# Attention in sets of four row groups, layer norm's deviations in two parts, and a load with a buffer for every piece

## The chip, the cores and the metric

The kernel runs on one core of one Trainium2 chip. The metric is the device time of one execution in microseconds. All arithmetic on the path here is in 32-bit floats, and a matmul of such operands appears in the profile as two records, one for each pass.

## The reference

The input x has 256 rows, 256 columns and 32 channels. Four layers follow each other, each preceded by a group norm over 16 groups of channels, and each adds its result to x.

```python
# layer 0: attention whose softmax weights sum to 1 over an axis that v lacks,
# so that what is left of it is the gated v
mn = (m - mu) * rsqrt(var + LN_EPS) * ln_gamma + ln_beta     # over the 32 channels
v = mn @ Wv                      # 32 -> 256
g = sigmoid(mn @ Wg)             # 32 -> 256
x = x + (g * v) @ Wo + bo
# layers 1 and 2: 3x3 mean, then the size of the Sobel gradient
x = x + sqrt(gx * gx + gy * gy + 1e-6)
# layer 3: two stacked LSTM-like cells with a group norm of their gates,
# along 256 time steps (the second axis) for 256 sequences (the first)
zz = group_norm(concat(z, h) @ W_cell + b_cell); i, f, o, g = split(zz)
c = sigmoid(f) * c + sigmoid(i) * tanh(g); h = sigmoid(o) * tanh(c)
x = x + (gn_x + z @ W_out + b_out)    # gn_x: x after its group norm, fed to the cells
```

## The kernel before

The image lies in SBUF as `xa`: 128 partitions are 4 columns of the image times 32 channels (the four "row groups" j of 32 partitions), and along the free axis there are 64 blocks of 256 rows of the image. Two blocks make a pair of 512 elements, `pair(t, k)`; there are 32 pairs k.

**Load** (L208 to L256). The image comes in eight pieces of 32 columns, each two DMAs of 512 KB on SP's queue into one of three `nat` buffers. PE transposes each into four PSUM tiles (L240), ACT copies them to `xa` (L247) and DVE takes the statistics (L248). Before the last piece's transposes PE computes the biases and the centred weights of `wv4` and `wg4` (L221, L233); these need the weights times gamma, which POOL computes (L230). POOL also fills `avg` (L193). In this part the order on each engine is the scheduler's: DMAs and small operations of later code (the recurrence's weights `wc`, a reduction L755) are moved forward into it. Group norm then aggregates the statistics (L159), averages them over channels with small matmuls, among junk matmuls (`busy`), and yields `less` (minus the mean) and the scale.

**Layer norm** (L281 to L337). Each pair is shifted by `less` into `xb`, half of them on DVE and half on POOL (L288). Eight groups g of four pairs follow: PE centres them with sixteen 32x32 matmuls (L306), ACT squares them (L316), and PE sums the squares of the group before into one bank `pvar` (L292). After the last group ACT takes the root (L322) and DVE its reciprocal, `rstd` (L324). Row k of it must be spread over 32 partitions for pair k. For pairs 0 to 2 a matmul does that (L334); for the others `rows_of` (L267) issues four DMAs on SP's queue, from one partition to 32 each, into one of four `rows` buffers, and POOL multiplies (`scaled`, L279).

**Attention** (L344 to L467). One step per pair k, 32 in all, written out by hand: `plan` gives each operation a time, the operations of all pairs are sorted by k times `step` plus that time, and each engine issues its own in that order. For every row group j and half u of the 256 outputs there are a `g` and a `v` matmul (L393, 32 rows by 128 columns of the array, so that four row groups can run side by side), a sigmoid `sg` on ACT (L402) and a product `mu` on DVE (L406) into a buffer `o`. Then `pr`, eight matmuls of 128 rows by 32 columns (L419), projects back; `r` adds the bias on ACT (L434), POOL adds to `xa` (L435), and `bn` takes statistics on DVE (L438). All PSUM tiles come from one list of eight free banks, taken in the order in which they were released; `sg` has 7 buffers and `o` 14. The centring of the recurrence's weights (L755 to L762) and `spread_out`, which calls `rows_of`, are strewn into the same order.

```python
todo = [
    (k * step + when, one_of, (o, u, j, k)) for k in range(NST) for when, o, u, j in plan
]
```

**The rest.** Two Sobel layers (L479) and the recurrence (L926) follow. The Sobel layers begin with a group norm that takes in junk matmuls too (L516). `RecurrentWeights.rest` (L716) loads the last small weights and computes a few selector columns on DVE (L734 to L743). Ahead of the recurrence there is a group norm with three junk matmuls before, two between and three after its two small matmuls, and then six more at `px` (L1107); after that come its first `zz` matmuls (L992, L995).

Of the kernel before, what the change touches and what calls it, by code (L numbers as in the profile page):

```python
# [33 lines left out]
K_GN, K_CEN = 0, 1  # L34
K_AVG, K_SOBEL = 0, 1
# [26 lines left out]
def net_kernel(  # L62
# [32 lines left out]
    xb = big2.tile([P, NB, S], F32, name="xb")  # L95

# [4 lines left out]
    kt = big2.tile([P, NK - 2, P], F32, name="kt")  # L101
    nc.scalar.dma_start(out=kt, in_=consts[:, 2:NK, :])
# [17 lines left out]
    gamma4 = per_channel(ln_gamma, "gamma4")  # L120
    beta4 = per_channel(ln_beta, "beta4")
# [3 lines left out]
    def four_times(w, n, name):  # L125
        t = big2.tile([P, n], F32, name=name)
        for j in range(J):
            nc.gpsimd.dma_start(out=t[j * C : (j + 1) * C, :], in_=w)
        return t

    wv4 = four_times(w_v, D, "wv4")
    wg4 = four_times(w_g, D, "wg4")
# [23 lines left out]
    def group_norm(stats, psum, before, after, rhs=None):  # L156
# [6 lines left out]
        busy(psum, 2, rhs)  # L163
# [27 lines left out]
    nc.gpsimd.memset(avg, 0.0)  # L191
    for g in range(GROUPS):
        nc.gpsimd.tensor_copy(avg[:, g, g, :], kt[:, K_AVG, 0:P:C])  # L193
    FIRST = 3
    spread = mp.tile([P, FIRST, P], F32, name="spread")
    nc.gpsimd.memset(spread, 0.0)
    for j in range(J):
        rows = slice(j * C, (j + 1) * C)
        nc.gpsimd.tensor_copy(
            spread[rows, :, rows],  # L200
            ident[rows, j * C : j * C + FIRST].unsqueeze(2).to_broadcast([C, FIRST, C]),
        )

    flag = cp.tile([1, 1], mybir.dt.int32, name="flag")
    stats = new_stats()
    WL = 32  # L208
    with tc.tile_pool(name="nat", bufs=3) as natp, tc.tile_pool(
        name="ps_in", bufs=4, space=PSUM  # L210
    ) as ps_in:
        norm_test(tc, natp, flag, gn_gamma, gn_beta)
        for w0 in range(0, T, WL):
            nat = natp.tile([P, 2, WL, C], F32, name="nat")
            for h in range(2):
                nc.sync.dma_start(out=nat[:, h], in_=x_nat[:, h, w0 : w0 + WL, :])
            if w0 == T - WL:
                pbias = ps_in.tile([P, 2, 2, P], F32, name="pt")
                for i, w in enumerate((wv4, wg4)):
                    for half in range(2):  # L220
                        nc.tensor.matmul(  # L221
                            pbias[:, i, half, 0:1],
                            lhsT=w[0:C, half * P : (half + 1) * P],
                            rhs=beta4[0:C, :],
                            start=True,
                            stop=True,
                        )
                nc.scalar.copy(wbias, pbias[:, :, :, 0:1].rearrange("p i h o -> p i (h o)"))
                for w in (wv4, wg4):
                    nc.gpsimd.tensor_scalar(w, w, gamma4, None, ALU.mult)  # L230
                    pw = ps_in.tile([P, 2, 2, P], F32, name="pt")
                    pw = pw[:, 0].rearrange("p h s -> p (h s)")
                    nc.tensor.matmul(pw, lhsT=kg[:, K_CEN, :], rhs=w, start=True, stop=True)  # L233
                    nc.scalar.copy(w, pw)
            for b2 in range(WL // (2 * J)):
# [12 lines left out]
                nc.vector.bn_stats(stats[:, blk // 2, :], dst)  # L248
# [5 lines left out]
        nc.vector.tensor_scalar(cen, kg[:, K_CEN, :], gn[0], None, ALU.mult)  # L254
        for w in (wv4, wg4):
            nc.scalar.activation(w, w, AF.Copy, scale=gn[0])  # L256

# [20 lines left out]
    with tc.tile_pool(name="lnq", bufs=12) as lnq:  # L281
# [47 lines left out]
        with tc.tile_pool(name="ps_sp", bufs=FIRST, space=PSUM) as ps_sp:  # L329
# [6 lines left out]
            for k in range(FIRST, FIRST + 3):  # L336
                scaled(k)  # L337
# [871 lines left out]
```

## Time and profile before

| | us |
|---|---|
| median of 3 runs | 2568.68 |
| lowest, highest | 2567.36, 2572.03 |
| profiled execution, its own time | 2571.38 |
| profiled execution, span | 2569.3 |

| stretch of the span | from, to |
|---|---|
| load | 0 to 38.9 |
| group norm | 38.9 to 45.4 |
| layer norm up to its last variance matmul | 45.4 to 67.1 |
| deviation, its reciprocal, first rows | 67.1 to 75.3 |
| attention | 75.3 to 348 |
| two Sobel layers | 348 to 602 |
| last group norm, start of the recurrence | 602 to 615 |
| recurrence | 615 to 2569 |

PE is busy 98% of the span, DVE 89%, ACT 88%, POOL 53%. A line of the profile gives the engine (PEld loads weights for PE; SPq, POOLq are queues), the line of the kernel, the tile written and the tiles read, shapes and durations. In brackets stands how long the engine sat idle before, and what it waited for.

### The profile page before, as it was taken

The page shows a single profiled execution, that of the slowest core. Times are in us where ns is not written, and L with a number is a line of the kernel's source. Part 1 is how long each engine was busy: PE and PEld are TensorE (multiplying, and loading weights), DVE is VectorE, ACT ScalarE, POOL GpSimd, SP SyncE. Part 2 cuts the span into 40 slices and gives each one's busy share as a digit, 9 for nine tenths or more (in the row PEclk, how much of TensorE's full clock was granted, in tenths as well). Part 3 has the DMA queues.
Part 4 walks back from the last instruction along what each step waited for, and adds up shares of the span by engine and source line. Part 5 has one row for each costly group of instructions (what it writes and reads, how often), then busy time and mean ns, then how long its engine had stood idle before and what let it go on. Part 6 is the DMA issues. An engine that isn't in the chain of part 4 may idle for free.

```text
span 2569.3 us, 41531 instructions
## 1 busy us (share of the span) xinstructions
PE 2510.2 (98%) x11605; PEld 1094.3 (43%) x11605; DVE 2274.3 (89%) x6623; ACT 2254.0 (88%) x6876; POOL 1350.1 (53%) x1387
## 2 busy tenths in 40 slices
PE   7899999998999999999999999999999999999997
PEld 4444445564444444444444444444444444444442
DVE  6577779796999999999999999999999999999996
ACT  5577757675999999999999999999999999999996
POOL 5233358683555555555555555555555555555553
PEclk9999999998999999999999999999999999999998
DMA  4776000002000101010101010100101010100000
GB/s 166 42 42 33 5 1 1 1 1 50 5 15 11 22 5 21 5 21 5 21 5 22 5 21 9 22 14 12 21 5 22 5 22 5 22 5 5 5 5 11
DMA packets 116441, 46.20 MB, mean 18 GB/s; under 512 B 76724, under 2 KB 109653, under 8 KB 116200
## 3 DMA queue, kind: packets, MB, share of 16 engines
q1 hardware_dynamic: 114020, 42.15, 11.7%
q8 instruction: 95, 1.56, 0.2%
q14 instruction: 146, 1.20, 0.2%
q10 hardware_dynamic: 1380, 0.99, 0.1%
q0 software_dynamic: 800, 0.30, 0.0%
HBM read 10.63 MB, written 8.39 MB: 7 GB/s over the span
## 4 chain that ended last, share of the span: by engine, by line
PE 96%; DMA 1%; DVE 1%; issue 1%; ACT 1%; POOL 0%; SPq 0%; DVEq 0%; POOLq 0%; ACTq 0%
PE zz L1027 36%; PE zz L1022 17%; PE zz L995 9%; PE pg L603 8%; PE pa L393 8%; PE pt L1079 5%; PE zz L992 3%; PE pa L419 2%; PE pt L1075 2%; PE px L1124 1%; PE px L1114 1%; PE pg L516 1%; DMA nat<-in_x_dram 1%; PE pc L306 0%; PE pvar L292 0%
## 5 line engine op out<-in xcount | busy, mean ns | idle before, releaser
L1043 POOL TENSOR_TENSOR rs<-ve,mhalf 128x4 f32<-128x4 f32 x1024 | 1031.0, 1007 | 922.7 <-DVE ve L1040 922.7
L1027 PE MATMUL zz<-wc,hT 128*128 128x512 f32 x2040 | 1059.4, 607 | 1.0 <-DVE hT L1085 1.0
L1016 ACT ACTIVATE ga<-zz,rs 128x128 f32<-128x128 f32 x3072 | 972.7, 377 | 39.3 <-POOL rs L1043 10.2
L1040 DVE TENSOR_REDUCE ve<-sq 128x4 f32<-128x516 f32 x1024 | 704.4, 688 | 29.2 <-ACT sq L1035 8.5
L1035 ACT ACTIVATE sq<-zz 128x512 f32<-128x512 f32 x1024 | 629.2, 614 | 38.5 <-PE zz L1027 16.3
L1022 PE MATMUL zz<-wc,hT 128*128 128x512 f32 x1024 | 525.0, 594 | 0.0
L1027 PEld LDWEIGHTS zz<-wc,hT 128*128 128x128 f32 x2040 | 328.6, 190 | 398.9 <-DVE c L1071 167.6
L1016 ACT ACTIVATE go<-zz,rs 128x128 f32<-128x128 f32 x1024 | 393.9, 385 | 0.0
L1063 DVE TENSOR_TENSOR c<-ga 128x128 f32<-128x128 f32 x1024 | 300.1, 293 | 61.8 <-ACT ga L1016 35.2
L1071 DVE TENSOR_TENSOR c<-c,fc 128x128 f32<-128x128 f32 x1020 | 288.9, 283 | 9.0
L1067 DVE TENSOR_TENSOR fc<-ga,c 128x128 f32<-128x128 f32 x1020 | 292.9, 287 | 2.7 <-ACT ga L1016 2.7
L995 PE MATMUL zz<-fx,xt 32*128 32x512 f32 x2048 | 265.6, 588 | 0.0
L402 ACT ACTIVATE sg<-pa,wbias 128x512 f32<-128x512 f32 x256 | 168.9, 687 | 89.5 <-PE pa L393 47.7
L406 DVE SCALAR_TENSOR_TENSOR o<-pa,wbias,sg 128x512 f32<-128x512 f32 x256 | 177.5, 746 | 60.5 <-PE pa L419 46.2
L1079 PEld LDWEIGHTS pt<-ident,c 128*128 128x128 f32 x512 | 71.0, 139 | 284.9 <-DVE c L1071 275.9
L393 PE MATMUL pa<-xb,wv 32*128 32x512 f32 x512 | 181.3, 615 | 8.7 <-DVE o L406 8.1
L393 PE MATMUL pa<-xb,wg 32*128 32x512 f32 x512 | 171.3, 638 | 0.8 <-DVE xb L335 0.8
L1082 ACT ACTIVATE th<-c 128x128 f32<-128x128 f32 x512 | 166.2, 325 | 0.4 <-DVE c L1071 0.4
L1082 ACT ACTIVATE th<-pt 128x128 f32<-128x128 f32 x512 | 145.9, 285 | 18.9 <-PE pt L1079 18.9
L1022 PEld LDWEIGHTS zz<-wc,hT 128*128 128x128 f32 x1024 | 161.2, 197 | 2.8 <-issue 0.5
L1085 DVE TENSOR_TENSOR hT<-pt,th 128x128 f32<-128x128 f32 x512 | 146.3, 286 | 15.8 <-ACT th L1082 15.7
L1075 PEld LDWEIGHTS pt<-ident,go 128*128 128x128 f32 x512 | 71.5, 140 | 202.5 <-ACT go L1016 202.0
(186 smaller groups left out, 2962.8 us busy)
## 6 DMA issues: line engine op xcount, KB each, us to landing
xt<-xa SPq DMA_DIRECT2D x256, 64.0 KB, 2.0
nat<-in_x_dram SPq DMA_DIRECT2D x16, 512.0 KB, 7.9
out_dram<-st SPq DMA_DIRECT2D x252, 32.0 KB, 1.7
rows<-rstd SPq DMA_DIRECT2D x116, 64.0 KB, 6.4
wc<-in_L_conv_W_cell_dram SPq DMA_DIRECT2D x2, 512.0 KB, 8.1
kt<-in_consts_dram ACTq DMA_DIRECT2D x1, 704.0 KB, 7.8
kg<-in_consts_dram ACTq DMA_DIRECT2D x1, 128.0 KB, 4.7
wv<-in_L_conv_Wv_dram POOLq DMA_DIRECT2D x4, 32.0 KB, 5.6
```

The lines of the kernel that those rows point to most:

```text
L393: nc.tensor.matmul(take((o, u, j, k)), lhsT=w[rows, u * P : (u + 1) * P], rhs=pair(xb, k)[rows], start=True, stop=True,)
L995: nc.tensor.matmul(v["zz", l, h, t], lhsT=inputs.of(t, r), rhs=fx[r, :], start=False, stop=l == 0 and t == 0,)
L1016: nc.scalar.activation(dst, gates(x, g), func, scale=scale)
L1022: nc.tensor.matmul(get("zz"), lhsT=v["hT", 0, t][:, seqs], rhs=wc[:, l, 0, :], start=False, stop=t == 0)
L1027: nc.tensor.matmul(get("zz"), lhsT=v["hT", l, t - 1][:, seqs], rhs=wc[:, l, 1, :], start=False, stop=True,)
L1035: nc.scalar.activation(sqs[l, h, t % 2][:, :, 0:H], four(get("zz")), AF.Square, scale=float(H**-0.5))
L1040: nc.vector.tensor_reduce(ve, sqs[l, h, t % 2], AX.X, ALU.add)
L1043: nc.gpsimd.tensor_tensor(rs, get("ve"), inputs.mhalf, ALU.pow)
L1063: nc.vector.tensor_mul(c, gates(get("ga"), 0), gates(get("ga"), 2))
L1067: nc.vector.tensor_mul(fc, gates(get("ga"), 1), get("c"))
L1071: nc.vector.tensor_add(c, c, get("fc"))
L1082: nc.scalar.activation(th, get("pt")[:, 1, 0:P] if turned else get("c"), AF.Tanh)
```

## The change

- **Load.** The image comes in two pieces of 16 and seven of 32 columns, each with a buffer of its own, all issued at once; `xb` is given the memory afterwards. Gamma, beta, `wv4` and `wg4` are loaded by SP after the fourth piece, `kt` and a separate `mean_of` after the last. POOL clears `avg`, fills it from `mean_of`, and then multiplies the weights by gamma. The weights' products (`weights`) come before the last two pieces. From here to the end of attention every engine issues in the order of the program text.
- **Group norm.** The chain is written out with fewer small operations; the pair 2 is shifted by ACT.
- **Layer norm.** DVE shifts all other pairs. The variance has two parts: groups 0 and 1, and groups 2 to 7. The deviation of the first is taken amid the squares of group 3, its reciprocal `rstds[0]` serves pairs 0 to 7, and rows 0 to 2 are sent at once, by DMA as all others; pair 0 is scaled by DVE. `spread` and its matmuls go. The test of gamma and beta (`norm_test`) moves here.
- **Attention.** A new plan with a step of 5.9 has `g` and `v` in sets of four row groups, the projection in two halves `pr` and `pb`, 8 buffers `sg`, 11 `o` and 3 `rows`; `spread_out` and `scaled` have other times. The weights of the recurrence are loaded after layer norm.
- **Seams.** The selector columns move into the first Sobel layer, the centring of the weights adds a negative mean in place of subtracting, and there are fewer junk matmuls ahead of the recurrence.

```diff
-    WL = 32
-    with tc.tile_pool(name="nat", bufs=3) as natp, tc.tile_pool(
-        name="ps_in", bufs=4, space=PSUM
+    front = ExitStack()
+    front.enter_context(tc.manual_schedule())
+    WIDTHS = [16, 16] + 7 * [32]
...
+        for i, wl in enumerate(WIDTHS):
+            name, bufs = ("nat", 7) if wl == 32 else ("half", 2)
+            nat = natp.tile([P, 2, wl, C], F32, name=name, bufs=bufs)
+            nats.append((nat, w0, wl))
             for h in range(2):
-                nc.sync.dma_start(out=nat[:, h], in_=x_nat[:, h, w0 : w0 + WL, :])
...
+                nc.sync.dma_start(out=nat[:, h], in_=x_nat[:, h, w0 : w0 + wl, :])
+            w0 += wl
+            if i == 3:
+                for t, v in ((gamma4, ln_gamma), (beta4, ln_beta)):
...
+                for t, w in ((wv4, w_v), (wg4, w_g)):
+                    for j in range(J):
+                        nc.sync.dma_start(out=t[j * C : (j + 1) * C, :], in_=w)
+        nc.sync.dma_start(out=kt, in_=consts[:, 3:NK, :])
+        mean_of = mp.tile([P, P], F32, name="mean_of")
+        nc.sync.dma_start(out=mean_of, in_=consts[:, K_AVG, :])
+        gb = norm_weights(tc, mp, gn_gamma, gn_beta)
+        nc.gpsimd.memset(avg, 0.0)
+        for g in range(GROUPS):
+            nc.gpsimd.tensor_copy(avg[:, g, g, :], mean_of[:, 0:P:C])
+        scaled_w = []
+        for w in (wv4, wg4):
+            scaled_w.append(mp.tile([P, D], F32, name="wgam", bufs=2))
+            nc.gpsimd.tensor_scalar(scaled_w[-1], w, gamma4, None, ALU.mult)
...
+            if i == len(nats) - 3:
+                weights()
...
+        less = small.tile([P, 1], F32, name="less")
+        nc.vector.tensor_scalar_mul(less, pm, -1.0)
...
+        busy(ps_gn, 3)
+        nc.scalar.activation(pair(xb, 2), pair(xa, 2), AF.Identity, bias=less)
+        gstd = small.tile([P, 1], F32, name="gstd")
+        nc.scalar.activation(gstd, pv, AF.Sqrt, bias=gn_eps)
+
+        def shifted(k):
+            nc.vector.tensor_scalar(pair(xb, k), pair(xa, k), one, less, ALU.mult, ALU.add)
+
+        shifted(0)
+        shifted(1)
...
+        nc.vector.tensor_scalar(cen, kg[:, K_CEN, :], scale, None, ALU.mult)
+        shifted(3)
...
+    EARLY = 2
+    rstds = [lnp.tile([P, 2 * S], F32, name=f"rstd{i}") for i in range(2)]
...
-            for k in range(NST):
-                e = nc.gpsimd if k % 2 else nc.vector
-                e.tensor_scalar(pair(xb, k), pair(xa, k), one, less, ALU.mult, ALU.add)
...
+                if g == 0:
+                    for k in range(J, NST - J):
+                        shifted(k)
                 sqs = []
-                for pc in pcs:
+                for j, pc in enumerate(pcs):
+                    if g == EARLY + 1 and j == 2:
+                        std = deviations()
+                        nc.vector.reciprocal(rstds[0], std)
+                        for k in range(3):
+                            rowsets[k] = rows_of(k)
+                        for k in range(NST - J, NST):
+                            shifted(k)
+                        norm_test(tc, mp, flag, gb)
+                        for k in range(3):
+                            scaled(k)
                     sqs.append(lnq.tile([P, 2 * S], F32, name="sq"))
                     nc.scalar.activation(sqs[-1], pc, AF.Square)
...
-    rw = RecurrentWeights(tc, cells, w_cell, b_cell)
+    rw = RecurrentWeights(tc, cells, one, w_cell, b_cell)
     stats = new_stats()
-    step = 6.6
+    step = 5.9000
     plan = [
...
+        (0.0000, "g", 1, 1),
+        (0.8334, "sg", 1, 1),
+        (2.9800, "g", 0, 1),
+        (3.7879, "sg", 0, 1),
+        (5.9100, "g", 1, 0),
+        (7.0264, "sg", 1, 0),
+        (7.4050, "g", 0, 0),
+        (8.3528, "sg", 0, 0),
+        (8.8600, "v", 0, 0),
+        (8.8700, "g", 0, 2),
+        (9.7954, "sg", 0, 2),
+        (10.3250, "v", 1, 2),
+        (10.3350, "v", 1, 1),
+        (10.3450, "v", 1, 0),
+        (10.3550, "g", 1, 3),
+        (10.5787, "mu", 0, 0),
+        (11.5740, "sg", 1, 3),
+        (11.5795, "mu", 1, 0),
+        (11.8200, "v", 0, 3),
+        (11.8300, "g", 1, 2),
+        (12.9473, "mu", 1, 1),
+        (13.2750, "v", 0, 1),
+        (13.2850, "g", 0, 3),
+        (13.2950, "v", 0, 2),
+        (13.9836, "sg", 1, 2),
+        (13.9933, "mu", 1, 2),
+        (14.0771, "mu", 0, 2),
+        (14.3106, "sg", 0, 3),
+        (14.4469, "mu", 0, 1),
+        (14.7500, "v", 1, 3),
+        (15.3906, "mu", 0, 3),
+        (16.2340, "mu", 1, 3),
+        (17.9944, "pr", 0, 0),
+        (19.6839, "pb", 0, 0),
+        (20.2213, "r", 0, 0),
+        (22.5883, "bn", 0, 0),
...
+            elif o in ("pr", "pb"):
+                half = o == "pb"
+                po = held["po", k][1] if half else take(("po", k))
+                for i in range(J):
+                    nc.tensor.matmul(
+                        po[i * C : (i + 1) * C, :],
+                        lhsT=wo[:, half, :],
+                        rhs=sbuf.pop(("o", half, i, k)),
+                        start=not half,
+                        stop=half,
+                    )
...
+        for k in range(3, NST):
+            todo.append(((k - 2) * step + 4.0, scaled, (k,)))
+            todo.append(((k - 5) * step + 4.5, spread_out, (k,)))
...
-    stats = sobel_layer(xa, xb, stats, 7, 16, [])
+    stats = sobel_layer(xa, xb, stats, 7, 16, [rw.selectors])
...
-        gn = group_norm(stats, ps_n, 3, 3)
+        gn = group_norm(stats, ps_n, 1, 0, 3)
...
-    at(-1e5, busy, 6)
+    at(-1e5, busy, 2)
```

`RecurrentWeights.__init__` stands unchanged in what it issues: two DMAs of 512 KB for `wc` on SP's queue, then POOL clears `bc`, then a DMA on SP's queue writes one row of it.

## The prediction

> **What bounds the kernel now.** I read the busy shares by stretch first: where does an engine run full, and where does none? Columns: stretch, length, then busy us of PE, PEld, DVE, ACT and POOL, the granted PE clock, DMA share, GB/s.
>
> ```profile
> 0.00:38.90 38.90, 25.72 (x141) 21.23 (x141) 22.82 (x36) 19.57 (x37) 19.05 (x52) 0.96 0.74 273
> 38.90:45.40 6.50, 3.94 (x18) 3.12 (x19) 5.74 (x14) 2.66 (x5) 3.05 (x4) 0.95 0.01 3
> 45.40:67.10 21.70, 21.65 (x320) 5.07 (x320) 11.12 (x13) 16.41 (x32) 11.76 (x13) 0.86 0.01 3
> 75.30:111.00 35.70, 27.47 (x148) 13.15 (x148) 16.77 (x27) 19.17 (x30) 8.83 (x7) 0.93 0.83 49
> 111.00:344.00 233.00, 232.49 (x1372) 108.68 (x1373) 180.55 (x267) 165.35 (x257) 79.08 (x76) 0.99 0.47 26
> 615.00:2560.00 1945.00, 1930.98 (x8242) 786.02 (x8242) 1806.25 (x5912) 1847.64 (x6175) 1031.00 (x1024) 1.00 0.07 13
> ```
>
> The recurrence (last row) is three quarters of the span and keeps its code; only its start is touched. So the change lives in the first 348 us. In attention PE looks full, but DVE and ACT are at 77% and 71%. Next, the waits there, and one step in order of time:
>
> ```profile
> DVE o L406 <- PE pa L419: 44.0, 28, 1.6
> ACT sg L402 <- DVE o L406: 40.2, 29, 10.3
> ...
> 201.87 4.89 DVE L406 SCALAR_TENSOR_TENSOR o<-pa,wbias,sg 128x512 f32<-128x512 f32 x7 [1.59 <-PE pa L419]
> 202.65 1.34 ACT L402 ACTIVATE sg<-pa,wbias 128x512 f32<-128x512 f32 x2 [1.08 <-DVE o L406]
> 207.10 0.74 DVE L406 SCALAR_TENSOR_TENSOR o<-pa,wbias,sg 128x512 f32<-128x512 f32 x1
> 207.76 0.68 DVE L438 BATCH_NORM_STATS2 stats<-xa 128x6 f32<-128x512 f32 x1
> 208.95 1.92 PE L419 MATMUL pa<-o,wo 128*32 128x512 f32 x16
> 210.03 4.89 DVE L406 SCALAR_TENSOR_TENSOR o<-pa,wbias,sg 128x512 f32<-128x512 f32 x7 [1.59 <-PE pa L419]
> ```
>
> Once a step DVE stops 1.59 us for the projection (L419). I counted the "o" buffers in program order: all 14 are held when "pr" comes, so the next "mu" needs the buffer that its first matmul frees, 1.08 us after it starts (208.95 to 210.03). Likewise "sg" waits 1.08 us for the first "mu" (201.87 to 202.65), as a count of 7 buffers taken in the order in which they are freed gives. That order of reuse is what I walk below. Last, the load's end and the deviations:
>
> ```profile
> 32.17 0.93 POOL L230 TENSOR_SCALAR wv<-wv,gamma 128x256 f32<-128x256 f32 x1 [8.35 <-issue]
> 34.65 3.52 PE L240 MATMUL pt<-ident,nat 128*128 128x128 f32 x16
> 36.80 2.73 DVE L248 BATCH_NORM_STATS2 stats<-xa 128x6 f32<-128x512 f32 x4 [3.20 <-ACT xa L247]
> ...
> L288 DVE TENSOR_SCALAR xb<-xa,one,less x16: 535/990/994, 42.3 to 55.5; 128x512 f32<-128x512 f32 x16
> ...
> 67.83 3.35 DVE L324 RECIPROCAL rstd<-std 128x512 f32<-128x512 f32 x1 [11.31 <-ACT std L322]
> ...
> 80.93 1.27 POOL L279 TENSOR_TENSOR xb<-xb,rows 128x512 f32<-128x512 f32 x1 [23.77 <-PE pa L393]
> 107.60 1.26 POOL L279 TENSOR_TENSOR xb<-xb,rows 128x512 f32<-128x512 f32 x1 [3.97 <-DMA rows<-rstd]
> ```
>
> The last transposes wait behind the weights' product, which waits for POOL. The first row set lands 9.7 us after its first DMA (71.21 to 80.93), each further one 5.3 us later (five in 26.67).
>
> **The change, part by part.** Times are us from the span's start, or from t0, the first centring matmul (45.43 now).
>
> **Load.** All nine pieces are now issued at once, the weights of the recurrence (1.05 MB) and "kt" come later, and at the 400 GB/s of the middle of the load the image would be in at about 25 us, ready at 29 instead of 39.5. But the front is now in program order. On POOL the "avg" copies stand ahead of the two gamma products, and they wait for "mean_of", which is queued on SP behind every piece and behind "kt". Bytes ahead of it: 9.5 MB, 24 us, plus 2.2 for the start and 1 to 1.5 for sixteen small DMAs put between the pieces: 27.5. Then eight copies 1.06 and two products 0.92 each: 30.45. "weights" stands on PE ahead of the last two pieces, so their transposes start at about 31.05, 0.6 after the product as now (34.06 to 34.65). One piece took 4.8 from there to its last statistic, a second adds 2.7: 38.6. Gain 0.9, not 10.
>
> **Group norm.** From last statistic (39.5) to t0 took 5.95. Out go the 0.6 of a weight reduction ahead of the aggregate, the copy of the mean, the bias, one shift ahead of "cen" (0.9) and the long "cen" (0.73 beside a POOL shift, about 0.25 alone). Left: 3.65. Gain 2.3.
>
> **Layer norm and first steps.** DVE now shifts alone. No row shows that alone: bounds are 0.42 (the 512-wide cast at 609.98) and 0.99 (beside POOL); I take 0.42, since POOL is now idle there. The 24 shifts queued ahead of the first reciprocal then end at t0+10.6, before the early deviation: its Square neighbours end 10.9 after t0 now, plus 0.69. Reciprocal to 14.9, row sets 0, 1, 2 at 24.6, 29.9, 35.2. PE waits for that deviation before its next variance, about 1.8, but ends at t0+23.5, under the rows. What follows is a new queue: POOL scales pair 2 (36.5), then clears "bc" (0.94), the "bc" DMA waits for that, and row set 3 stands behind it on SP. Four issues 1.8, landing 6.4, scale 1.3: t0+47.3. Pair 3's first matmul stands ahead of the first projection: t0+47.8. Now it is t0+46.95. Loss 0.9. The 8.2 us between layer norm and attention are thus not won, but turned into a wait for rows. Costed at nothing under that wait: the norm test on DVE (3.9: L695 twice 0.68, reduction 2.27, cast 0.14), the second reciprocal (3.35) and the sigmoid table load (1.3); with rows earlier they would show, 3 us at most, since the first "mu" comes late. At 0.99 a shift it would be 13 us worse.
>
> **Attention step.** Constants from the trace: "mu" to "mu" 0.69, "bn" 0.65; "mu" start to a freed bank or buffer 0.77; "sg" start to its "mu" 0.73; a set of four matmuls on four row groups holds PE 0.86 (two passes of 0.43), its result is there at 1.07; last pass to the other tiling 0.57; half a projection the same. With eight "sg" buffers taken in the order freed, the steady order of the new plan gives, with "mu" 0,0 of the next pair at 0: bn 0.69; mu 1,0 1.34; mu 1,1 2.03. Then sg 1,2 takes the buffer that mu 1,1 frees: 2.82, so mu 1,2 starts at 3.55 and not at 2.72. PE: set A ends with the bank freed at 0.77, first half of the projection 1.77, set B 2.77 to 2.85; its result 3.92 is in time for mu 0,2 at 4.24. sg 0,3 takes mu 0,2's buffer at 5.02, so mu 0,3 comes at 5.76 (not 5.62). Set C 4.9 feeds mu 1,3 at 6.45 and mu 0,0 at 7.14. With rounding of the intervals 7.11 a step. The eleven "o" buffers never fill: ten are held at "pr". So the projection's stop goes, and two hand-overs from DVE to ACT and back (0.83 and 0.14) come in its place above DVE's own 6.2. First to last projection is 252.0 now (92.4 to 344.4); 31 x 7.11 = 220.4. Gain 31.6. The row sets need 5.3 a step, POOL 3.1; both fit. Three row buffers for four cost nothing: a set is issued when the third one before it is used, three steps (21) ahead, and needs 9.7. The weights' centring stays 0.6 a piece on POOL, with another form of the same operation.
>
> A rule speaks against this part: the Trainium skill, "TensorEngine Tiling (Array Packing)", Key Properties, has a change of tiling mode drain the array. Halves make four changes a step out of two. By the row, 202.09 to 202.64, a change costs 0.12 over the 0.43 of a pass: 0.5 a step. By the rule with the full 0.59 pass and a 0.16 weight load it is 0.32, two of them ahead of set B, where there is 0.32 of slack: 0.1 a step, 3 us in all. I take the row.
>
> **End and seams.** The last pair's projection half is shorter: 0.7. The selector operations leave the seam to the Sobel layer: 0.3. At the recurrence, four junk matmuls fewer around group norm and four fewer at "px" bring the first "zz" from 612.71 to 610.4, a gain of 2.3 by these rows. But "TensorE: Matmul & The Clock Gate", What's actually happening, has the array at half clock until about 3.4 us of activity; here too the clock was 0.50 at 602 to 604 and full only after three us of junk. Then set L824 (1.9) runs at half clock behind junk that is slower as well: gain gone, down to -1.5. I take 0.5.
>
> **Sum.** 0.9 + 2.3 - 0.9 + 31.6 + 0.7 + 0.3 + 0.5 = 35.4. The profiled execution took 2571.4 (span 2569.3), so 2536.0; it stands 2.7 above the median of the runs, so 2533.3.
>
> **Rivals.** *Smoother than walked* (0.20): "sg" hand-overs overlap and the step is near DVE's 6.2 to 6.4, 25 us more; if "mean_of" also lands early, up to 8 more: 2500 to 2516. For it: ACT needs under 6 a step. Against: the present trace obeys the buffer order exactly. *Shallower* (0.14): shifts nearer 0.54 to 0.99, or a step of 7.5 to 7.9 by a third hand-over or PE's conflicts: 2543 to 2562. *Slower* (0.04): ACT and DVE become a relay. Each "sg" that waits for the "mu" just before its own adds 0.83 to 6.17; the present 8.13 plus the other gains (3.8 over 31 steps) is passed at 8.25, that is from the third hand-over at full price on (8.66, 2581). I count one and a part. *The change does nothing net* (0.02): the step stays near 8.1 because the bank pool, not "o", is what held it. Against: the 1.08 fits the buffer to 0.01.
>
> **How the numbers follow.** Likeliest case 0.60: 2533, of itself 2524 to 2545 (step 6.9 to 7.4, "mean_of" 1.5 either way, seam -1.5 to +2.3). Leaving out the best third of the smoother case and the worst third of the shallower leaves 2508 to 2556. A measurement here tells 0.2%, some 5 us, from no change. Faster 0.94, same 0.02, slower 0.04.
>
> **What would show it.** Right: PE idle from about 22 to 29 with POOL waiting for "mean_of"; statistics ending near 38.6; PE waiting for rows up to t0+47; steps of 7.1 with an "sg" waiting for a "mu" twice a step, no stop of DVE at the projection. Wrong: statistics done at 30, steps under 6.6 or over 7.6, a shift over 0.55, or a recurrence longer than now.

## The result, and the profile after

| | us |
|---|---|
| before, median of 4 runs | 2568.75 (2567.36 to 2572.03) |
| after, median of 4 runs | 2545.06 (2544.43 to 2546.56) |
| ratio, 95% interval | 0.9907 (0.989 to 0.9924) |
| after, profiled execution, its own time | 2544.43 |
| after, profiled execution, span | 2542.6 |

The gain is 23.7 us where the forecast had 35.4. The stages of the two profiled executions show where they part. t0 is again the first centring matmul, 45.43 before and 51.28 after.

| stretch | before | after | gain | forecast |
|---|---|---|---|---|
| start to the load's last statistic | 39.5 | 47.2 | -7.7 | +0.9 |
| to t0 | 5.9 | 4.1 | +1.8 | +2.3 |
| t0 to first projection | 46.95 | 51.2 | -4.25 | -0.9 |
| first projection to first Sobel aggregate | 256.7 | 219.5 | +37.2 | +32.3 |
| two Sobel layers | 253.0 | 251.5 | +1.5 | +0.3 |
| last aggregate to first `sq<-zz` | 12.1 | 15.7 | -3.6 | +0.5 |
| recurrence and end | 1955.2 | 1953.4 | +1.8 | 0 |

The gains add up to 26.7, the difference of the spans. Before's profiled execution took 2.6 more than its median, after's 0.6 less than its own, which is the rest but for 0.2 between span and device time. So attention gave more than forecast, and the load, the way to the first projection and the seam to the recurrence lost 15.6, where the forecast had the three at +0.5. (The 1.5 of the Sobel layers need not be the change's: e5 below, which has the Sobel code of before, takes 124.1 for the first layer, before 125.8, after 124.3.)

The busy shares by stretch, with the columns of the forecast's first view:

```profile
0.00:47.20 47.20, 26.65 (x145) 23.53 (x146) 20.52 (x32) 20.75 (x37) 8.91 (x30) 0.82 0.55 203
47.20:51.28 4.08, 3.27 (x16) 2.37 (x15) 3.28 (x9) 2.01 (x6) 0.00 (x0) 1.00 0.00 0
51.28:76.00 24.72, 19.63 (x320) 4.79 (x320) 19.66 (x34) 19.51 (x37) 0.00 (x0) 1.00 0.31 18
76.00:102.50 26.50, 21.99 (x68) 10.35 (x68) 12.90 (x16) 10.42 (x16) 4.67 (x4) 0.58 0.78 74
111.00:316.00 205.00, 205.00 (x1402) 82.93 (x1398) 178.92 (x269) 167.25 (x260) 78.88 (x79) 1.00 0.63 34
590.00:2533.00 1943.00, 1929.77 (x8234) 785.70 (x8238) 1806.39 (x5911) 1847.28 (x6174) 1030.91 (x1024) 1.00 0.07 13
```

In attention DVE's share rises from 77% to 87%: this is the gain. The load is longer, at a DMA share of 0.55 where it was 0.74. From 76 to 102.5 DVE, ACT and POOL are busy less than half of the time, and PE 83% of it at a granted clock of 0.58. Attention's list of waits (total, times, longest), from 111 to 300 us:

```profile
ACT sg L441 <- DVE o L445: 26.0, 31, 0.9
...
DVE o L445 <- ACT sg L441: 18.7, 23, 0.8
DVE o L445 <- PE pa L432: 3.3, 4, 0.8
```

DVE in order of time, over one step:

```profile
218.68 4.23 DVE L445 SCALAR_TENSOR_TENSOR o<-pa,wbias,sg 128x512 f32<-128x512 f32 x6 [0.81 <-ACT sg L441]
222.83 0.68 DVE L477 BATCH_NORM_STATS2 stats<-xa 128x6 f32<-128x512 f32 x1
223.43 1.39 DVE L445 SCALAR_TENSOR_TENSOR o<-pa,wbias,sg 128x512 f32<-128x512 f32 x2
225.63 4.23 DVE L445 SCALAR_TENSOR_TENSOR o<-pa,wbias,sg 128x512 f32<-128x512 f32 x6 [0.81 <-ACT sg L441]
```

ACT's two sigmoids that wait, of this step and the next:

```profile
219.53 1.28 ACT L441 ACTIVATE sg<-pa,wbias 128x512 f32<-128x512 f32 x2 [0.88 <-DVE o L445]
226.48 1.28 ACT L441 ACTIVATE sg<-pa,wbias 128x512 f32<-128x512 f32 x2 [0.88 <-DVE o L445]
```

A step is 225.63 - 218.68 = 6.95, and from first to last projection 6.94 on average. The stop of 1.59 at the projection is gone; from 111 us on no long wait of DVE names the projection (L458). In its place stands one hand-over a step, in both directions: DVE's product waits 0.81 for a sigmoid, and ACT's next sigmoid waits 0.88 for the buffer that this product frees (218.68 to 219.53). The load, first SP's queue in order of time:

```profile
2.62 1.88 SPq L200 DMA_DIRECT2D nat<-in_x_dram  x4
4.55 4.08 SPq L205 DMA_DIRECT2D gamma<-in_L_conv_ln_gamma_dram  x4
9.65 4.36 SPq L205 DMA_DIRECT2D beta<-in_L_conv_ln_beta_dram  x4
14.05 1.82 SPq L210 DMA_DIRECT2D wv<-in_L_conv_Wv_dram  x4
15.92 1.81 SPq L210 DMA_DIRECT2D wg<-in_L_conv_Wg_dram  x4
17.77 5.59 SPq L200 DMA_DIRECT2D nat<-in_x_dram  x10
```

The waits of the small transfers in that queue's list up to 60 us:

```profile
SPq L205 <- DMA nat<-in_x_dram: 4.1, 4, 1.1
SPq L205 <- DMA half<-in_x_dram: 1.4, 1, 1.4
```

POOL in order of time at the end of the load:

```profile
36.16 1.05 POOL L217 COPY avg<-mean_of 128x4 f32<-128x4 f32 x8 [29.16 <-DMA mean_of<-in_consts_dram]
37.21 0.92 POOL L221 TENSOR_SCALAR wgam<-wv,gamma 128x256 f32<-128x256 f32 x1
38.13 0.91 POOL L221 TENSOR_SCALAR wgam<-wg,gamma 128x256 f32<-128x256 f32 x1
```

The sixteen small transfers hold SP's queue from 4.55 to 17.77: those of `wv` and `wg` take 0.46 each to issue (1.82 for four), and among those of gamma and beta are five waits, 5.5 in all, for the landing of pieces issued before. Only then are the other ten transfers of the image issued. `mean_of` lands at 36, POOL multiplies the weights after it, and the last two pieces are transposed behind that.

### The profile page after: what moved, and what is told of

It is laid out like the page before. It is cut to its first block, busy times and chain, and to the rows that moved or that the text cites. A ratio compares the mean times of both kernels' runs of the same rounds, so it can differ in the third digit from the quotient of the medians.

```text
span 2542.6 us, 41402 instructions
## 1 busy us (share of the span) xinstructions
PE 2478.7 (97%) x11567; PEld 1064.8 (42%) x11567; DVE 2275.0 (89%) x6635; ACT 2256.8 (89%) x6878; POOL 1324.9 (52%) x1352
## 4 chain that ended last, share of the span: by engine, by line
PE 94%; DMA 2%; DVE 1%; SPq 1%; ACT 1%; POOL 0%; issue 0%; POOLq 0%; DVEq 0%; ACTq 0%
PE zz L1072 36%; PE zz L1067 17%; PE zz L1040 9%; PE pg L639 9%; PE pa L432 6%; PE pt L1124 5%; PE zz L1037 3%; PE pa L458 2%; PE pt L1120 2%; PE px L1169 1%; PE px L1159 1%; PE pg L552 1%; DMA nat<-in_x_dram 1%; SPq L306 1%; DMA rows<-rstd 1%; DVE xb L285 1%
## 5 line engine op out<-in xcount | busy, mean ns | idle before, releaser
L441 ACT ACTIVATE sg<-pa,wbias 128x512 f32<-128x512 f32 x256 | 167.5, 686 | 56.4 <-DVE o L445 30.7
L445 DVE SCALAR_TENSOR_TENSOR o<-pa,wbias,sg 128x512 f32<-128x512 f32 x256 | 177.7, 744 | 31.6 <-ACT sg L441 20.7
L432 PE MATMUL pa<-xb,wg 32*128 32x512 f32 x512 | 167.0, 665 | 7.8 <-DVE xb L316 4.1
L1130 DVE TENSOR_TENSOR hT<-pt,th 128x128 f32<-128x128 f32 x512 | 146.3, 286 | 15.9 <-ACT th L1127 15.7
L432 PE MATMUL pa<-xb,wv 32*128 32x512 f32 x512 | 157.4, 651 | 0.0
```

Source lines behind the costliest of these rows:

```text
L432: nc.tensor.matmul(take((o, u, j, k)), lhsT=w[rows, u * P : (u + 1) * P], rhs=pair(xb, k)[rows], start=True, stop=True,)
```

## The experiments

All but e5 start from the kernel after. Their line numbers move with the edits: in e9, e11 and e12 the reduction of `bc` (L795) is L808 or L809, and the product (L445) is L457 or L460. In the text "us less" is against its median of 2545.1. Each ratio is to the kernel before, run on the same chip. Its median was 2567.9 to 2570.5 in those groups of runs, so that differences of 2 us between runs of different groups say nothing.

**e1: ten sigmoid buffers.**

```diff
-                sg = sbuf["sg", u, j, k] = atp.tile([P, 2 * S], F32, name="sg", bufs=8)
+                sg = sbuf["sg", u, j, k] = atp.tile([P, 2 * S], F32, name="sg", bufs=10)
```

> The kernel after with ten sigmoid buffers (sg) instead of eight, so that by the order of freeing no sigmoid takes the buffer that the product just before it frees. Theory A (the steady step of 6.95 us is the buffer hand-over from DVE to ACT and back, 0.81 + 0.88): the hand-over goes, the next bound is the loop of banks and the projection's half, 3.92 + 4 x 0.69 = 6.68 a step, 30 steps x 0.27 = 8 us less: 2537. Theory B (DVE's own 6.2 us would bind at once): 23 us less, 2522. Rival C (something else holds the step, the bank pool or PE): 6.95 as before and 2545, no change.

Measured: 2538.1 (ratio 0.9882, 0.9865 to 0.9898), 7.0 less. DVE in order of time:

```profile
213.33 4.21 DVE L445 SCALAR_TENSOR_TENSOR o<-pa,wbias,sg 128x512 f32<-128x512 f32 x6 [0.63 <-ACT sg L441]
...
220.09 4.21 DVE L445 SCALAR_TENSOR_TENSOR o<-pa,wbias,sg 128x512 f32<-128x512 f32 x6 [0.63 <-ACT sg L441]
```

The step is 6.76. ACT no longer waits for a product but for a matmul ("ACT sg L441 <- PE pa L432: 32.6, 56, 1.2" in its list of waits). Theory A holds: the hand-over of buffers set the step. That the loop of banks, forecast at 6.68, is next fits the size and the new wait, but was not tested by itself. First projection to first aggregate fell from 219.5 to 213.0, or 6.5.

**e5: the kernel before with one more `o` buffer.**

```diff
-                gated = sbuf["o", u, j, k] = atp.tile([P, 2 * S], F32, name="o", bufs=14)
+                gated = sbuf["o", u, j, k] = atp.tile([P, 2 * S], F32, name="o", bufs=15)
...
-                    r = atp.tile([P, 2 * S], F32, name="r", bufs=2)
+                    r = atp.tile([P, 2 * S], F32, name="r", bufs=1)
```

> The kernel before with fifteen buffers for the gated products (o) instead of fourteen, paid for by one buffer instead of two for the projection's copy (r). Theory A (DVE's stop of 1.59 us a step is the wait for the buffer that the projection's first matmul frees): the stop shrinks to about 0.9, the step goes from 8.0 to about 7.34, 31 steps x 0.66 = 20 us less: 2548. Rival B (the bank pool or the projection itself holds DVE, the buffer only happens to fit): the stop stays at 1.59, the step at 8.0, the time at 2569. A longer step than 8.1 would be the single r buffer.

Measured: 2551.2 (0.9921, 0.9905 to 0.9938), 18.6 less than before. DVE in order of time:

```profile
201.79 4.23 DVE L406 SCALAR_TENSOR_TENSOR o<-pa,wbias,sg 128x512 f32<-128x512 f32 x6 [0.84 <-PE pa L419]
...
209.14 4.23 DVE L406 SCALAR_TENSOR_TENSOR o<-pa,wbias,sg 128x512 f32<-128x512 f32 x6 [0.67 <-PE pa L419]
```

The step is 7.35, the stop 0.67 to 0.84. So the stop of 1.59 in the kernel before was the wait for the buffer, as the forecast counted it, and the rival by which the bank pool held it is ruled out. One buffer alone brings the step more than halfway to that of the whole new plan, and these 18.6 us are more than three quarters of the 23.7 that the whole change won.

**e6: the projection's halves at one place.**

```diff
-        (19.6839, "pb", 0, 0),
+        (17.9945, "pb", 0, 0),
```

> The kernel after with both halves of a projection put at one place of the plan (17.99), so that PE changes its tiling twice a step and not four times and all eight projection matmuls of a set run on end. Theory A (the halves matter: set B is then ready 0.86 us later and DVE stops for it once a step): step 6.95 to about 7.5, 31 x 0.54 = 16 us more, 2561. Rival B (the sigmoid hand-over covers it, the halves bring nothing by themselves): step 6.95, 2545. Rival C (each change of tiling costs PE time that counts): shorter, by at most 4 changes x 0.12 = 0.5 us a step less two, so 31 x 0.24 = 7 us, 2538.

Measured: 2566.2 (0.9986, 0.998 to 0.9993), 21 more: nearly all that the change had won. DVE in order of time:

```profile
215.95 3.57 DVE L445 SCALAR_TENSOR_TENSOR o<-pa,wbias,sg 128x512 f32<-128x512 f32 x5 [0.73 <-PE pa L432]
...
222.25 0.75 DVE L445 SCALAR_TENSOR_TENSOR o<-pa,wbias,sg 128x512 f32<-128x512 f32 x1 [0.81 <-ACT sg L441]
223.73 3.57 DVE L445 SCALAR_TENSOR_TENSOR o<-pa,wbias,sg 128x512 f32<-128x512 f32 x5 [0.73 <-PE pa L432]
```

The step is 7.78. The hand-over (0.81) stays, and a second stop of 0.73 for the late set comes beside it. Theory A had the mechanism, at 0.54 a step where it costs 0.83. Rival C is out: two changes of tiling fewer do not make the kernel faster. What a change costs by itself e6 cannot tell, since the later set covers it; the trace of the kernel after can (below).

**e2, e3, e4: the load.** e2 puts the gamma products first on POOL; e3 moves the small transfers to POOL's queue; e4 does both.

```diff
+        scaled_w = []
+        for w in (wv4, wg4):
+            scaled_w.append(mp.tile([P, D], F32, name="wgam", bufs=2))
+            nc.gpsimd.tensor_scalar(scaled_w[-1], w, gamma4, None, ALU.mult)
         nc.gpsimd.memset(avg, 0.0)
         for g in range(GROUPS):
             nc.gpsimd.tensor_copy(avg[:, g, g, :], mean_of[:, 0:P:C])
-        scaled_w = []
...
```

```diff
-                        nc.sync.dma_start(out=t[j * C : (j + 1) * C, :], in_=w)
+                        nc.gpsimd.dma_start(out=t[j * C : (j + 1) * C, :], in_=w)
```

(The loop over gamma and beta is changed in the same way.)

> The kernel after with POOL's two gamma products put ahead of the clearing and the eight copies of avg, which wait for mean_of. Theory A (weights on PE waits for POOL, which waits for mean_of to land at 36.0): last statistic of the load at about 36 instead of 47.2 (last piece lands near 32.3, plus 3.8), 11 us less: 2534. Rival B (PE, cold after its pause, or the transposes themselves set the end): last statistic at 44 or later, gain under 3 us.

> The kernel after with the sixteen small transfers of gamma and beta issued by POOL's queue instead of SP's; the order of everything else is kept. Theory A (on SP each small transfer waits for the landing of a piece issued eight before it, which leaves the DMA engines at a share of 0.13 to 0.25 from 12 to 18 us and mean_of late): no such gap, mean_of lands near 27.5 as forecast, last statistic near 38.6, 8.6 us less: 2536.5. Rival B (the pieces are limited by the DMA engines anyway): mean_of at 33 or later, last statistic at 44 or later, gain under 3 us.

> Both edits of the load in one: gamma products first on POOL and the sixteen small transfers on POOL's queue. Theory A (the two causes add up): last piece lands near 25.5, last statistic near 29.5 to 34, 13 to 17.7 us less: 2527 to 2532. Rival B (either edit alone frees the same wait, so that the second brings nothing): as the better of the two alone, about 2534. Theory A is told from B by the last statistic: under 34 or near 36.

| | time | ratio, interval | `avg` copies start | last statistic ends | us less |
|---|---|---|---|---|---|
| after | 2545.1 | 0.9907 | 36.2 | 47.2 | |
| e2 | 2536.5 | 0.9873 (0.9857 to 0.989) | 36.3 | 38.9 | 8.6 |
| e3 | 2538.5 | 0.9877 (0.9861 to 0.9894) | 30.1 | 40.8 | 6.6 |
| e4 | 2529.3 | 0.9847 (0.9831 to 0.9864) | 30.1 | 32.6 | 15.7 |

The stretch from 12 to 18 us in the kernel after:

```profile
12.00:18.00 6.00, 4.87 (x28) 4.63 (x26) 4.74 (x8) 4.49 (x8) 0.00 (x0) 1.00 0.18 50
```

The same stretch of e4:

```profile
12.00:18.00 6.00, 6.00 (x40) 6.00 (x39) 4.63 (x7) 4.72 (x9) 4.21 (x9) 1.00 1.04 398
```

All three theories A hold in kind, e2 and e3 some 2 us short of their sums, and the two causes add up (8.6 + 6.6 = 15.2 for 15.7). With one cause gone the last statistic ends at 38.9 or 40.8, near the 39.5 of the kernel before; only with both gone, at 32.6, is the new load worth something. The DMA share between 12 and 18 us goes from 0.18 to 1.04, so the pieces were late because SP was held, not because the DMA engines were full. SP waits in e4 too: its twelfth transfer is issued at 8.29 (8.32 in the kernel after), and each further one 1.1 to 2.0 later. But there every transfer that is let in is a large one, where in the kernel after it was a small one, and the engines ran dry. With e3 alone `mean_of` lands at about 30 and not at 27.5, the other part of the forecast's miss; e2 ends 2.9 later than expected.

**e8: `bc` cleared on DVE.**

```diff
-        nc.gpsimd.memset(self.bc, 0.0)
+        nc.vector.memset(self.bc, 0.0)
```

> The kernel after with the clearing of bc on DVE instead of POOL, so that the bc transfer and row set 3 behind it on SP do not wait for POOL's scaling of pair 2. Theory A (that queue sets the first projection, as the forecast had it): row set 3 is issued near 84 and pair 3 scaled near 94 instead of 99.1, first projection 4 to 5 us earlier (98), time 2541. Rival B (the row sets are paced by the DMA engines, 5.3 us each, and pair 3 can only be scaled 5.3 us after pair 2): first projection 1 us earlier at most, 2544.

Measured: 2540.3 (0.988, 0.9863 to 0.9896), 4.7 less. Pair 3 is scaled at 96.2 with t0 at 52.0, that is t0+44.2 for t0+47.9, and the first projection starts at t0+47.8 for t0+51.2. The 3.4 lie nearer to A than to B. (In the seven traces in which the code from t0 to here is that of the kernel after, the first projection lies between t0+49.6 and t0+51.2, so that the edit's own share is 1.8 to 3.4.) But DVE's rows in order of time hold, in the kernel after, a wait that neither theory named:

```profile
76.67 3.35 DVE L377 RECIPROCAL rstd<-std 128x512 f32<-128x512 f32 x1
90.42 0.68 DVE L795 TENSOR_REDUCE bm<-bc 33x4 f32<-33x512 f32 x1 [10.41 <-DMA bc<-in_L_conv_b_cell_dram]
91.03 1.39 DVE L445 SCALAR_TENSOR_TENSOR o<-pa,wbias,sg 128x512 f32<-128x512 f32 x2
```

DVE's first product of attention stands behind the reduction of `bc`, and that waits 10.41 for the transfer, while the first sigmoid had started at 80.17. In e8 `bc` is issued earlier too: the wait is 7.36, and the first product comes at t0+37.6 instead of t0+39.75. So e8 does not tell the row sets from `bc`. In the kernel before, the transfer of `bc` was issued at 26.7, right behind the image's last, and the reduction did not wait.

**e9: pairs 0 to 2 spread by TensorE again.** The core of the edit:

```diff
+            for k in range(FIRST):
+                pb = ps_sp.tile([P, 2 * S], F32, name="pb")
+                nc.tensor.matmul(pb, lhsT=spread[:, k, :], rhs=rstds[0], start=True, stop=True)
+                nc.vector.tensor_mul(pair(xb, k), pair(xb, k), pb)
...
-                        for k in range(3):
+                        for k in range(FIRST, FIRST + 3):
                             rowsets[k] = rows_of(k)
```

> The kernel after with pairs 0 to 2 scaled from rows spread by TensorE, as in the kernel before, out of the early deviation as soon as layer norm's matmuls are done, and the row sets of pairs 3 to 5 sent in the place of those of 0 to 2. Theory A (the row sets through DRAM are what the first projection waits for): pair 0 is scaled at t0+26, pairs 1 and 2 within 2 us, row set 3 lands near t0+25, so the first projection is near t0+39 instead of t0+51.2, 12 us less: 2533. Rival B (the next wait is right behind: DVE's norm test and second reciprocal, 7.3 us, and PE's slow stretch at the start of attention): first projection at t0+46 to t0+49, 2 to 5 us less: 2541.

Measured: 2540.4 (0.9883, 0.9868 to 0.9898), 4.7 less; first projection at 99.2 with t0 at 50.8, so t0+48.4. Three pairs are scaled by 75.8 and two more row sets land by 80. (The row sets go from SBUF to SBUF; "through DRAM" in the expectation is a slip.) DVE in order of time:

```profile
75.69 3.35 DVE L389 RECIPROCAL rstd<-std 128x512 f32<-128x512 f32 x1
...
87.75 0.68 DVE L808 TENSOR_REDUCE bm<-bc 33x4 f32<-33x512 f32 x1 [8.71 <-DMA bc<-in_L_conv_b_cell_dram]
88.35 1.39 DVE L457 SCALAR_TENSOR_TENSOR o<-pa,wbias,sg 128x512 f32<-128x512 f32 x2
```

Rival B has the size right but not the wait: it is not the norm test or the reciprocal, but `bc` again. With the rows early, the first projection comes only 2.8 sooner, and the first product is 2.2 sooner (t0+37.5) because `bc` lands sooner. Its transfer stands on SP behind the first twelve row transfers and the weights `wc`. e12 tests that.

**e7: the junk matmuls put back ahead of the recurrence.**

```diff
-        gn = group_norm(stats, ps_n, 1, 0, 3)
+        gn = group_norm(stats, ps_n, 3, 2, 3)
...
-    at(-1e5, busy, 2)
+    at(-1e5, busy, 6)
```

> The kernel after with the junk matmuls of the kernel before put back around the last group norm (3, 2, 3 for 1, 0, 3) and px (6 for 2). Theory A (the seam to the recurrence lost 3.6 us because fewer junk matmuls leave TensorE at half clock): clock 1.00 by some 6 us after the last aggregate in every execution, first sq<-zz at 12 to 12.5 us after it, 3 us less: 2541.5. Rival B (junk stands in the way of real matmuls, as the forecast's sum had it): 2.3 us more, 2547. Rival C (the clock at that place depends on when a slow stretch happens to begin, not on the junk): first sq<-zz at 12 to 16 us, the time within 1 us of 2545.

Measured: 2541.6 (0.989, 0.9873 to 0.9906), 3.4 less. Its stretches from the last aggregate on, at 573.2:

```profile
573.00:575.00 2.00, 2.00 (x8) 1.62 (x6) 1.22 (x2) 0.00 (x0) 0.00 (x0) 0.53 0.50 100
575.00:578.00 3.00, 3.00 (x14) 2.58 (x13) 1.15 (x8) 0.92 (x2) 0.00 (x0) 0.75 0.49 100
578.00:582.00 4.00, 3.66 (x19) 1.80 (x17) 2.44 (x7) 1.51 (x3) 0.00 (x0) 1.00 0.50 102
```

Those of the kernel after, whose last aggregate is at 573.5:

```profile
573.00:579.00 6.00, 5.20 (x15) 3.68 (x15) 2.74 (x10) 1.21 (x2) 0.00 (x0) 0.50 0.49 99
579.00:585.00 6.00, 4.34 (x12) 1.44 (x12) 2.21 (x5) 1.21 (x3) 0.00 (x0) 0.50 0.51 103
585.00:590.00 5.00, 4.05 (x10) 1.55 (x10) 0.85 (x3) 0.60 (x1) 0.00 (x0) 0.50 0.49 99
```

With the junk the clock is back at 1.00 at 576.5, 3.3 us after the aggregate, and the first `sq<-zz` comes 12.25 after it instead of 15.7; the matmuls of `pg` (L869) take 3.68 in the kernel after and took 1.93 before. Theory A holds for this execution, and all traces here together show how A and C share the effect. Ahead of the aggregate PE stands idle for 3.1 us (569.8 to 572.9 in the kernel after). From the aggregate to the first `sq<-zz`:

| | clock falls before the aggregate | clock falls later or not at all |
|---|---|---|
| few junk matmuls | 15.7 (after, e2, e3, e8, e9) | 12.5 to 12.8 (e1, e4, e6: falls 5 us after the aggregate) |
| junk as before | 12.1, 12.25 (before, e7) | 11.0 (e5, e10, e11, e12: does not fall here) |

Where the clock falls differs between executions, as C has it; with the junk the stretch is 1.5 to 3.6 shorter in either case, as A has it. The gain of 3.4 is not all from here, either: of the 3.5, 1.4 were lost again, since the second Sobel layer up to the aggregate took 128.6 for 127.2, and 1.3 came from an earlier first projection.

**e10, e11, e12: the edits together.** e10 has e1, e4, e7 and e8; e11 has e9's edit in the place of e8's; e12 adds to e11 that `bc` is cleared on POOL and loaded on SP behind the image:

```diff
         nc.gpsimd.memset(avg, 0.0)
...
+        bc = cells.tile([KX, L, G], F32, name="bc")
+        nc.gpsimd.memset(bc, 0.0)
+        nc.sync.dma_start(out=bc[C : C + 1], in_=b_cell.rearrange("(o l) m -> o l m", o=1))
         for g in range(GROUPS):
...
-        self.bc = cells.tile([KX, L, G], F32, name="bc")
-        nc.gpsimd.memset(self.bc, 0.0)
-        nc.sync.dma_start(out=self.bc[C : C + 1], in_=b_cell.rearrange("(o l) m -> o l m", o=1))
+        self.bc = bc
```

> The kernel after with five of the single edits at once: gamma products first, small transfers on POOL's queue, bc cleared on DVE, ten sg buffers, junk matmuls put back. Theory A (the stages follow one another, so the single gains add up: load 15.7, bc 4.7, sg 7.0, junk 3.4 by the measured medians): 30.8 us less than 2545.1, that is 2514. Rival B (a wait freed in one stage is taken up by the next, the row sets above all): 2520 to 2526.

> The same with the spread by TensorE of pairs 0 to 2 and the early row sets of 3 to 5 in the place of the bc edit. Theory A (all add up, with 12 us for the rows in place of 4.7): about 2507. Rival B (the rows bring no more than the bc edit once the load ends early): about 2514.

> The kernel of e11 with bc cleared on POOL and its transfer issued on SP behind the load, ahead of layer norm, instead of behind the first twelve row transfers and the recurrence's weights. In e11 the first gated product on DVE stands behind the reduction of bc, which waits 9.24 us for that transfer and starts at 74.4, while its sigmoid is there at 66. Theory A (this wait, not the row sets, is what set the first projection in the kernel after, in e9 and in e11): no wait of DVE for bc, the first product starts near 66 instead of 75, first projection near t0+41 instead of t0+49, 8 us less than e11's 2517.3: 2509. Rival B (the row sets or TensorE's half clock at the start of attention take over at once): first projection at t0+46 or later, 3 us less at most, 2514 to 2517.

| | time | ratio, interval | t0 | first projection |
|---|---|---|---|---|
| after | 2545.1 | 0.9907 (0.989 to 0.9924) | 51.3 | t0+51.2 |
| e10 | 2515.4 | 0.9791 (0.9777 to 0.9804) | 36.5 | t0+46.6 |
| e11 | 2517.3 | 0.9796 (0.9783 to 0.981) | 36.9 | t0+49.0 |
| e12 | 2509.4 | 0.9767 (0.9754 to 0.978) | 37.1 | t0+40.2 |

e10 adds up (29.7 for 30.8). e11 does not, as its rival said, and e12 shows why. DVE in order of time in e11:

```profile
74.40 0.68 DVE L808 TENSOR_REDUCE bm<-bc 33x4 f32<-33x512 f32 x1 [9.24 <-DMA bc<-in_L_conv_b_cell_dram]
75.00 1.39 DVE L457 SCALAR_TENSOR_TENSOR o<-pa,wbias,sg 128x512 f32<-128x512 f32 x2
```

DVE in order of time in e12, the same two operations:

```profile
65.26 0.62 DVE L809 TENSOR_REDUCE bm<-bc 33x4 f32<-33x512 f32 x1
68.67 1.41 DVE L460 SCALAR_TENSOR_TENSOR o<-pa,wbias,sg 128x512 f32<-128x512 f32 x2 [2.79 <-PE pa L447]
```

With `bc` there early the first projection comes 8.8 sooner against t0, and the time is 7.9 less than e11's, as theory A had it. Of the 8.8, 6.5 lie ahead of the first product. The other 2.3 lie behind it, where the clock is 0.50 in e11 (69.0 to 86.1) and 1.00 in e12; whether the clock fell in e11 because of `bc` is not shown. e12 is 35.7 us faster than the kernel after and 58.5 faster than before, and the best version here.

## Why the forecast was right, and where its sum was wrong

**Attention step: right, and a little too careful.** The buffer count that carried it is shown by e5 (7.34 expected, 7.35 measured) and by e1 (6.68 and 6.76). The walk gave 7.11; 6.95 was measured. Of the two hand-overs that it placed in a step, the first is there at its price (0.81 for 0.83); the second, 0.14, does not show. 31 x 0.16 is 5.0, which is about the 4.9 by which first projection to aggregate beat its term.

**The weighed rule on changes of tiling.** The row (0.12 a change) was taken over the rule of the Trainium skill, "TensorEngine Tiling (Array Packing)", Key Properties. The trace of the kernel after bears the row out. A set's second pass and the projection's half behind it:

```profile
218.59 0.59 PE L432 MATMUL pa<-xb,wv 32*128 32x512 f32 x1
219.13 1.06 PE L458 MATMUL pa<-o,wo 128*32 128x512 f32 x8
```

The other tiling starts 0.54 after the pass before it, less than the 0.59 that this pass takes and 0.11 over the 0.43 of a pass. (The set's own two passes, at 218.06 and 218.59, stand 0.53 apart, so that the change may cost less still.) A drain of the size that the prediction weighed, 0.32, does not show.

**Load: the term that failed.** The forecast let sixteen small transfers between the pieces cost "1 to 1.5"; they held SP for 13.2 us (4.55 to 17.77). "`mean_of` at 27.5" became 36.0, and all that was hung on it held: the copies 1.05, the products 0.92 each, the transposes 1.1 behind them for 0.6, the last statistic at 47.2, 8.6 later than the 38.6 forecast. The order on POOL, by which the weights wait for `mean_of`, was read rightly (e2); the pace of the queue ahead of it was not (e3). About 2.5 us of it stay open, since in e3 `mean_of` still lands at 30 and not at 27.5.

**Group norm: right.** 3.65 forecast from last statistic to t0, 4.08 measured.

**Layer norm: right. First steps: the wrong wait.** The shifts start 0.46 apart for 0.42 taken (23 in 10.59); the 0.54 that one takes alone stood in the prediction's own line as its least (535). PE's wait for the early deviation is 1.84 for 1.8; the reciprocal ends at t0+14.3 for 14.9; pairs 0, 1 and 2 are scaled at t0+24.8, 29.5 and 35.6, for row sets at 24.6, 29.9 and 35.2. Then pair 3's scaling starts 1.9 late: from its first issue the set took 9.8, as the first set of the kernel before had (9.7), and not the 8.2 of the sum. But this is not what held the first projection, as the forecast had it. PE waited only 0.25 for pair 3:

```profile
100.46 1.22 PE L432 MATMUL pa<-xb,wg 32*128 32x512 f32 x2 [0.25 <-POOL xb L316]
```

Until then it was busy, at a clock of 0.50 since 90.75, with matmuls held up by DVE's products, and these had waited 10.41 for `bc`. Eleven products come before the first projection, and it follows the first of them after 11.45 in the kernel after, 10.1 in e8, 10.85 in e9 and e11, 8.6 at full clock in e12. The first product comes at t0+39.75, 37.6 in e8, 37.5 in e9 and 31.6 in e12, as `bc` lets it. So t0+47.8 lay near the measured 51.2 by luck: the rows were forecast well, but the forecast had no term for the wait that counts. It put the clearing of `bc` in SP's way and did not see that DVE waits for the same tile. The early deviation won nothing in the kernel after (t0+51.2 for 46.95 before); with the rows of e9 and `bc` early it is t0+40.2 (e12). An early `bc` without e9's rows was not run.

**Seam to the recurrence: the direction was wrong.** The forecast weighed +2.3 (less junk in the way) against -1.5 (half clock) and took +0.5; the profile has -3.6, and by the table under e7 the same code gave -0.4 to -0.7 in three other executions. The half clock cost more than its bound, since not only `pg` but the whole stretch from before the aggregate on ran at 0.50, up to 602.7, in the recurrence. Behind it stands the rule that spoke against the step, "TensorE: Matmul & The Clock Gate", What's actually happening: the array stays at half clock until a window of about 3.4 us was busy. With the junk the traces agree: the full clock came back 3.4 us after it had fallen, in before (601.15 to 604.6) and in e7 (573.15 to 576.55). In the kernel after they do not show it: PE was busy without a gap by the profile from 578.5 to 583.1, 4.6 us, and stayed at 0.50. What counts as busy stays open. The same section says that the window runs freely and does not start with the kernel; no run here shows where it starts.

**Cases.** The time, 2545, lies at the upper end of the likeliest case (2524 to 2545) and where the shallower case was put, but not by the latter's mechanism: the shifts were not slow and the step was shorter than walked. That it lies there is in part luck: by stretch, -8.6 for the load, -3.4 for the first steps and -4.1 for the seam stand against +4.9 for attention. The relay of the slower rival did not come: one hand-over a step, not three.

## What to carry to other kernels

Count what a queue must issue, and not only its bytes: here sixteen small transfers in front of ten large ones cost 6.6 us (e3). When a transfer is moved later in a queue, look through the program order of every engine for what waits on it; here it was a small reduction on DVE, and all products stood behind it. Where two waits lead to the same operation, ask which ends last there: PE's wait for rows was 0.25, and taking the rows away (e9) showed little until the other wait went too. A stop once a step could be told here from the count of buffers in the order in which they come free, and one more buffer tested it.

## What the runs showed of the hardware

- Transfers on SP's queue took 0.46 us each to issue (four of `wv`, 32 KB each, in 1.82; four of the image, 512 KB each, in 1.88). Small ones waited for the landing of large ones issued earlier (five waits, 5.5 us in all, in the kernel after). This fits at most eight open at a time: the twelfth transfer of the queue waited for a piece of the first four, the next four for the four pieces behind those. No run tested the number. The DMA engines stood at a share of 0.18 meanwhile.
- TensorE stayed at half clock from 572.0 to 602.7 in the kernel after, while the profile had PE busy about 80% of the time (13.6 of 17 us from 573 to 590), once for 4.6 us without a gap; in e7 and in the kernel before, the full clock came back 3.4 us after it had fallen, under unbroken matmuls.
- A change between 32x128 and 128x32 tiling cost at most 0.11 us over a pass in the kernel after (218.59 to 219.13, a pass 0.43).
- DVE's shift of 128x512 next to an idle POOL took 0.54 alone and started every 0.46 in a row; beside POOL it took 0.99.
